# A decoder layer on one core: loads at the start split and reordered, the filter transformed by halves, and a new hand-found order

## The chip, the cores and the metric

The kernel runs on 1 core of a Trainium2 chip. The metric is the time of one execution on the device in microseconds (us), as the median of several runs; less is better.

## The reference

The input x has 4 batches of 1024 tokens of 256 values. The layer is a Hyena block, a cross attention with 16 heads over 64 context tokens, and a feed-forward block with ternary weights, each followed by a layer norm. What matters here is the Hyena block; `h` is a filter of full length for each of 2 orders and 256 channels:

```
t = linspace(0, 1, L)[:, None]                       # L = 1024
pe = sin(t * bands * 10)                             # 33 bands
h = sin(10 * (pe @ w1.T + b1)) @ w2.T + b2           # 64 hidden, 2 * 256 out
h = (h * exp(-exp(filt_decay) * t) + filt_bias) / L  # per order and channel
u = depthwise_conv3(x @ w_in.T + b_in)               # 768 channels: x0, x1, v
for n in range(2):
    y = irfft(rfft(v, 2L) * rfft(h[n], 2L))[:L]      # a long causal convolution
    v = y * u[n]
out = v.T @ w_out.T + b_out
```

## The kernel before, in words

**Units.** The Hyena part works on 8 units, a batch and a half of the 256 channels each (`units`, u = 0 to 7). Per unit: three projections (`stage_j`, which calls `project`: PE multiplies x by columns of `w_in`; ACT writes the middle tap of the three-tap convolution and the two outer taps into a pair of `tap` tiles; two adding DMAs issued by POOL put the outer taps onto the middle one). There are two pairs of tap tiles, so the third projection reuses the pair of the first, after its DMAs. Then `stage_tv` and `stage_tx` transpose on PE, `stage_f` transforms v by matmuls with the matrix `fw`, `stage_p` multiplies by the transformed filter `hf` on DVE, and `stage_i0`, `stage_i1` go back with the matrix `gi_`. `stage_f` takes one of two ways: the direct one, or *by fourths*, where `fourths` multiplies with a quarter of the matrix, and `join` makes the rest out of sums and differences on DVE. Which units go by fourths is the set `FOUR`. Attention and feed-forward follow from about 340 us on.

**The filter.** Before unit 0 can multiply, the filter must be there. `filter_basis`: two matmuls of 512 columns into `z`, a chain of seven DVE operations on `arg` and `kk` (64 partitions x 1024) that brings the argument of the sine into range, eight Exp on ACT for the decay (`dspace`, from the loaded `fdb`), one Sin into `saug`. `filters`: for each of eight pieces of 128 steps a matmul (`hp`), a multiplication and an addition on DVE (`hsb`). Then the transform: steps 0, 1, 4, 5 (even modulo 4) go by `fourths` and `join` in two halves of 256 columns (a half is one order); steps 2, 3, 6, 7 go directly, 16 matmuls of 512 columns, a copy on ACT and an addition and a subtraction on DVE for each quarter; a last operation (`stt`, the sign step) adds the even part to the odd. All fp32 matmuls appear in the profile as two MATMUL instructions each.

**PSUM.** `big1` hands out four slots of 1024 columns in a ring, in the order of the program's text. A later user of a slot waits until all readers of the earlier one are done.

**The order.** The kernel's calls are held as `Step`s and issued in an order which `plan` finds on the host: it keeps a clock for each engine with estimated costs (`Step.cost`), and among the steps that could start next on an engine it takes the one with the least rank. A rank is the place in the text (`nc.at`), an offset by stage, and a number out of the table `RANKS`, one for each task, a run of steps with the same stage and place. Queues are in order: each engine and each DMA queue (SP, ACT, POOL) executes what was issued first. Before the change all work ahead of the first loop is one task.

**The first loads.** On SP's queue: w1T, pv, x of batch 0 in two loads of 512 KB, then dftf into `fw`, dfti into `gi_` (1 MB each). On ACT's queue: peT, the first row of filt over 128 partitions (256 KB, into `vf`), all of w_in (768 KB), w2T, the second row of filt, w_out.

In the profile `pv`, `w_in`, `xt`, `fw`, `hf` go by their own names; the tiles `arg`, `kk`, `saug`, `hsb` lie in `x1sp`, the loaded filt and w2T in `vf`, the decay in `q`, `pe_sb` in `x1sp`, w1 in `pr`. All lines are L87, the line of the helper that issues the steps, so groups are told apart by tile names.

Of the kernel before, what the change touches and what calls it, by code (L numbers as in the profile page):

```python
# [16 lines left out]
P = 128  # L17
# [9 lines left out]
CALM = set(range(4))  # L27
MAGIC = 12582912.0
# [61 lines left out]
class Step:  # L90
# [23 lines left out]
    def cost(self):  # L114
# [23 lines left out]
        if self.engine == "ACT":  # L138
            return 0.1 + n * 0.00098 + 0.15 * (self.sum is not None), 0.15
        if self.what == "tensor_copy":  # L140
            return 0.1 + n * 0.00096, 0.06
        if n == 16:
            return 0.22, 0.06
        return 0.52 + n * 0.001 * (n > 64), 0.06
# [75 lines left out]
class Clock:  # L220


    def __init__(self, steps, before):
        self.steps, self.before = steps, before
        self.free = dict.fromkeys(("PE", "DVE", "ACT", "POOL", "SP"), 0.0)
        self.table, self.mode, self.wire = None, "", 0.0
        self.bank = [dict.fromkeys(self.free, 0.0) for _ in range(8)]
        self.end, self.start = [0.0] * len(steps), [0.0] * len(steps)
# [17 lines left out]
    def run(self, i, ready):  # L246
# [9 lines left out]
        end = t + s.us  # L256
        self.free[e] = self.end[i] = end
# [58 lines left out]
def follow(steps, before, order):  # L316
# [10 lines left out]
    43.1, -121.95, -51.3, 35.7, 0.75, -46.25, -78.7, 6.05, -35.75, 2.2, 13.15, -82.8, 19.9, -102.2, -24.45, -20.9,  # L327
    3.9, -39.65, 15.15, -30.9, 40.2, -28.15, -4.8, -32.9, -66.5, -63.2, 15.35, -47.35, -49.85, -1.05, 11.9, 113.35,
    -71.55, -36, 0.4, 18.1, 20.7, -127.8, -32.2, -163.5, -136.8, -61, -75.2, 2.45, 13.25, -16.05, 2.55, -56.1,
    29.55, 38.35, 49, -27.05, 39.65, 24.25, 1.1, 49.95, -15.6, -95.2, -44.2, -50.7, -61.1, 3.4, -50.4, -36.55,  # L330
    -45.15, 10.05, 50.2, -68.15, 14.9, -46.8, -12.85, 9.45, -18.3, 7.8, -61.5, -13.95, 16.55, -82.75, -45.55, -3.85,
    -89.85, -61.3, 65.3, -109.05, -50.75, -85.6, 17.3, -26.7, -34.85, 37.55, 22, 64, 30.8, 6, -89.45, -67.35,
    -66.05, -121.9, -45.1, -22.4, -9.75, -88, -44.25, -38.1, -22.55, -6.65, 0.85, -94.4, -15.8, -40.2, 43.1, 15,
    5.2, 4.85, 27.75, 35.05, -26.4, 13.2, 33.35, 95.6, 17.8, -0.25, 27.75, -79.9, -121.9, -56.85, 54.45, -47.5,
    -52.1, 9.4, -71.7, -5.25, -19.5, -27.4, -22.5, -19.45, -30.15, -32.9, 3.3, -56.15, 22.3, -16.55, 37.25, 12.15,
    -6.2, 96.55, -79.6, -76.7, -57.45, -14.4, -29.75, -38.3, -50.25, -98, -79.45, -33.2, -16.8, -11.9, -30.4, -30.85,
    -38.35, -4.95, -51.25, -58.15, -10.35, 9.7, -38.05, -6.35, -30.75, -7.75, -13.8, -13.95, -27.9, -10.3, -9.6, -12.25,
    -8.9, -10.3, 27.45, 21.55, -7.65, -38.25, -4.65, 36.05, -3.9, 44.25, -9.1, 42.95, -79.9, 29.45, -4.3, 24.9,
    -5.75, -3.9, -46.4, 13.5, -0.3, -1.55, -5.35, -2.55, -2.75, -1.1, 44.9, -1.5, 39, -32.4, -4, -2.9,
    -0.55, -4.6, -31.9, -0.45, -39.05, 14.05, -0.7, 1.35, -1.05, -12.9, 3.6, -0.5, -0.45, 120.35, 0.8, 0.95,  # L340
    2.65, 0.65, 4.95, -0.5, 29.3, 3.55, 1.55, -69.05, 1.35, 0, -37.8, -11.2, -8.45, -9.8, 5.5, 17.85,
    -1.8, -13.1, 1.25, -1.45, -0.6, -40.15, -0.65, -0.1, 24.55, -0.1, -6.75, -53.3, -1.35, -16.75, 0.85, 0.55,
    40.95, 0.95, -10.9, 0.65, -66.2, -33.15, 0.4, 1.2, 16.45, 5.35, -4.3, 0.35, 0.9, -5.85, 9.45, 15.75,
    12.75, 9.2, 35.5, -36.65, -5.45, 0.9, 1, -7.85, 0.05, -2.75, -3.15, 24.65, -31, -2, 1.3, -9,
    0.6, -0.3, 0.5, 53.1, 87.6, -0.35, -1.15, 1.2, -8.75, 0.35, 15.4, -30.5, 45.1, -0.45, -2.85, -4.6,
    -0.4, -78.8, 2.05, 12.05, 63.1, 57.45, 49.85, 19.35, 15.8, -1.35, -0, 15.55, 6.6, 60.3, 26.35, -1,
    -54.85, 12.05, -1.5, -30.8, -14.5, 22.3, 56.65, 34.75, 2.75, 0.2, -0.35, 4.9, 3.6, 45.6, -6.4, 27.8,
    -40.95, 3.65, -43.65, 7.4, 5, 37.8, 73.2, 8.35, 20.9, -15.55, 13.7, -65.45, -48.75, 18.7, 37.55, 30.55,
    -0.5, 2.9, -29.2, -48.75, -33.8, 38.9, 13.4, 0.85, -40.6, 5, -115.8, -43.15, -7.95, 12.5, 107.55, 26.3,
    -32.5, 21.85, -8.5, 8.4, -2.6, -13, 33.15, -29.25, -63.15, 23.55, 10.35, -63.55, -57.75, 4, 84.3, -53.25,  # L350
    -10, -73.5, -73.55, 17.65,
# [7 lines left out]
def decoder_kernel(  # L359
# [152 lines left out]
    def big1(name):  # L512
        return space_of["rest"]()

    if True:
# [9 lines left out]
        def load_x(b):  # L525
            xts[b] = xt_t.rearrange("p (k l) -> p k l", k=2)
            for kt in range(2):
                nc.sync.dma_start(xts[b][:, kt, :], xT[kt * P : kt * P + P, b * L : b * L + L])
# [9 lines left out]
        pe_sb, arg, kk, saug = spare[3][:33], spare[0][:64], spare[1][:64], spare[2][:65]  # L538
# [7 lines left out]

        nc.sync.dma_start(w1_sb, w1T)
        nc.scalar.dma_start(pe_sb, peT)
        nc.sync.dma_start(pv, pvec)
        load_x(0)  # L550
# [3 lines left out]
        nc.scalar.dma_start(w_in_sb, w_inT.rearrange("(k p) f -> p k f", p=P))  # L554
        nc.scalar.dma_start(w2_sb, w2T)
        nc.scalar.dma_start(fdb[:, 1, :], fd[:, 1, :])
        nc.sync.dma_start(fw, dftf.rearrange("(k p) f -> p k f", p=P))
# [11 lines left out]
        def filter_basis():  # L569
            z = big1("z")  # L570
            for h in range(2):
                mm(z[:64, h * 512 : h * 512 + 512], w1_sb, pe_sb[:, h * 512 : h * 512 + 512], start=True, stop=True)
            ts_(arg, z[:64, :], pv[:64, C_B1 : C_B1 + 1], 10.0, ALU.add, ALU.mult)
# [9 lines left out]
            act(saug[:64, :], arg, AF.Sin)  # L583

        def filters():

            hsb = [spare[4 + t // 2][:, t % 2 * 512 : t % 2 * 512 + 512] for t in range(8)]
# [5 lines left out]
            for half in range(2):  # L593
                n2 = slice(2 * half, 2 * half + 2)
                c2 = slice(256 * half, 256 * half + 256)
                ps = fourths(f"ha{half}", lambda par, q: hsb[4 * par + q][:, c2])
                h = hf[:, n2, 0]
                join(h.rearrange("p n c (s k d) -> p s c k n d", s=2, k=2), h[:, :, :, 0:256], h[:, :, :, 256:512], *ps)

            for cs in range(2):  # L600
                for kt in range(2):
                    m = (2 * cs + kt) * P
                    ha = big1(f"ha{cs}_{kt}")
                    for par in range(2):
                        for q in range(2):
                            mm(
                                ha[:, par * 512 : par * 512 + 512],
                                fw[:, 2 * par + q, m : m + P],
                                hsb[4 * par + 2 + q],
                                start=q == 0,  # L610
                                stop=q == 1,
                            )
                    ho = hospace[:, 2 * cs + kt]
                    nc.scalar.copy(ho, ha[:, 512:1024])

                    sg = C_SG + (cs + kt) % 2
                    for st, op in ((0, ALU.add), (1, ALU.subtract)):
                        f = slice(st * 256 + kt * P, st * 256 + kt * P + P)
                        h1, h0 = hf[:, :, 1, cs, f], hf[:, :, 0, 1 - cs, f]
                        tt_(h1, ha[:, 0:512].rearrange("p (n d) -> p n d", d=P), ho.rearrange("p (n d) -> p n d", d=P), op)  # L620
# [882 lines left out]
```

## Time and profile before

| | us |
|---|---|
| median of 3 runs | 681.19 (680.97 to 683.53) |
| the profiled execution, its own time | 683.8 |
| its span, first to last instruction | 682.0 |
| TensorE matmul (PE) busy | 629.3 |
| VectorE (DVE) busy | 605.2 |
| ScalarE (ACT) busy | 413.5 |
| GpSimd (POOL) busy | 201.9 |

The mean granted TensorE clock is 0.983 of full speed. The page gives each engine's busy time over the span; the same by stretches shows where in the span an engine is idle. The chain that ended last follows the work back from the last instruction to what released it. A group of instructions is told by engine, operation and tiles, with the number of instructions, the busy time and the mean length of one. Lengths of matmuls overlap, since they are pipelined: the distance from one to the next is shorter than the length.

### The profile page before, as it was taken

The numbers are of one execution on the slowest core, as the hardware profiler recorded it, in microseconds if no ns is written. First come the engines' busy times: TensorE is split into PE (matmuls) and PEld (weight loads), VectorE is DVE, ScalarE is ACT, GpSimd is POOL, SyncE is SP. The second block draws the span as 40 slices with busy tenths as digits, with TensorE's granted clock in tenths as the row PEclk, the third lists the DMA queues.
The fourth block names the chain that finished last, engine by engine and source line by source line (L and its number), as shares of the span: only waits on it lengthen the run. The fifth ranks groups of instructions, "written<-read, shape, count | busy, mean of one in ns | idle before, by whom it ended". The sixth has DMA issues, their size and how long they took to land.

```text
span 682.0 us, 12320 instructions
## 1 busy us (share of the span) xinstructions
PE 629.3 (92%) x4731; PEld 432.0 (63%) x4764; DVE 605.2 (89%) x1214; ACT 413.5 (61%) x626; POOL 201.9 (30%) x303
## 2 busy tenths in 40 slices
PE   4989799999999989999799998999999999999973
PEld 1445377777787667875577666756566666656642
DVE  4469859999989989999899899879998989989997
ACT  4623446538256855387132342598988898788871
POOL 1300313204132313374001224223333333533344
PEclk9989899999999989999799999999999999999999
DMA  8563848649596496965833130001211113413145
GB/s 279 97 105 123 169 83 149 124 98 183 120 166 113 69 209 113 172 115 100 187 116 83 51 62 2 3 16 33 48 40 40 41 48 50 93 48 56 40 78 131
DMA packets 65487, 65.71 MB, mean 96 GB/s; under 512 B 36660, under 2 KB 47284, under 8 KB 65430
## 3 DMA queue, kind: packets, MB, share of 16 engines
q0 software_dynamic: 17472, 35.66, 30.2%
q1 hardware_dynamic: 46044, 26.26, 14.8%
q10 hardware_dynamic: 1914, 3.02, 1.4%
q8 instruction: 37, 0.61, 0.4%
q14 instruction: 20, 0.16, 0.1%
HBM read 17.21 MB, written 4.19 MB: 31 GB/s over the span
## 4 chain that ended last, share of the span: by engine, by line
PE 61%; DVE 23%; DMA 5%; issue 4%; ACT 4%; POOL 2%; ACTq 0%; POOLq 0%; DVEq 0%
PE ps_t L87 61%; DVE t L87 5%; DVE q L87 5%; DVE small_t L87 4%; DMA xc<-tap 3%; DVE vf L87 2%; DVE xt L87 2%; DVE x1c L87 2%; DMA w_in<-in_w_inT 2%; ACT tap L87 1%; POOL ln_t L87 1%; DVE x1sp L87 1%; DVE ln_t L87 1%; ACT x1sp L87 1%; POOL small_t L87 1%
## 5 line engine op out<-in xcount | busy, mean ns | idle before, releaser
L87 PE MATMUL ps_t<-hf 128*128 128x512 bf16 (+1 forms) x479 | 98.4, 322 | 11.4 <-DVE x1c L87 3.8
L87 PE MATMUL ps_t<-xt,w_in 128*128 128x512 f32 (+1 forms) x200 | 90.8, 600 | 6.5 <-DMA w_in<-in_w_inT 5.4
L87 PE MATMUL ps_t<-vt,fw 128*128 128x256 f32 x384 | 90.9, 387 | 4.0 <-ACT tap L87 2.9
L87 POOL DMA_DIRECT2D xc<-tap x32 | 39.2, 1226 | 169.0 <-ACT tap L87 131.0
L87 PEld LDWEIGHTS ps_t<-vt,fw 128*128 128x128 f32 x384 | 72.9, 193 | 18.9 <-ACT tap L87 3.6
L87 PEld LDWEIGHTS <-hf 12*128 12x128 bf16 (+2 forms) x768 | 56.5, 97 | 40.0 <-issue 18.1
L87 DVE TENSOR_TENSOR t<-vf,hf 128x1024 f32<-128x1024 f32 x64 | 76.3, 1219 | 0.0
L87 ACT ACTIVATE tap<-ps_t,tbias,pv 128x1024 f32<-128x1024 f32 x48 | 55.9, 1209 | 20.7 <-DMA xc<-tap 20.7
L87 PEld LDWEIGHTS ps_t<-xt,w_in 128*128 128x128 f32 x200 | 38.2, 195 | 47.1 <-issue 43.6
L87 DVE TENSOR_TENSOR t<-t 128x1024 f32<-128x1024 f32 (+1 forms) x60 | 57.3, 973 | 1.5 <-DMA t<-q 1.4
L87 PE MATMUL ps_t<-q,gi__108 128*128 128x256 f32 x192 | 48.8, 401 | 6.6 <-DVE q L87 3.4
L87 PE MATMUL ps_t<-gi__108,q 128*128 128x256 f32 (+1 forms) x256 | 50.3, 352 | 1.7 <-DVE q L87 1.7
L87 POOL TENSOR_TENSOR small_t<-small_t,mhalf 128x1 f32<-128x1 f32 x64 | 35.8, 566 | 46.8 <-DVE small_t L87 46.4
L87 PEld LDWEIGHTS ps_t<-gi__108,q 128*128 128x128 f32 x256 | 43.9, 201 | 8.2 <-DVE q L87 2.1
L87 ACT ACT_TABLE_LOAD x34 | 43.6, 1283 | 7.2 <-DMA pv<-in_pvec 5.5
L87 PEld LDWEIGHTS ps_t<-q,gi__108 128*128 128x128 f32 x192 | 36.8, 200 | 17.6 <-DVE q L87 6.0
L87 PE MATMUL ps_t<-tap,hf 128*32 128x128 f32 (+1 forms) x896 | 44.3, 260 | 0.3
L87 DVE TENSOR_TENSOR q<-t 128x512 f32<-128x512 f32 x64 | 44.2, 730 | 0.1
L87 DVE TENSOR_REDUCE xt<-ps_t 128x16 f32<-128x1024 f32 x32 | 38.9, 1216 | 5.4 <-PE ps_t L87 3.9
L87 POOL COPY vf<-vf 128x1024 f16<-128x1024 f16 x32 | 33.2, 1038 | 29.6 <-DMA hf<-vf 10.3
L87 ACT ACTIVATE xc<-ps_t,cbias,pv 128x512 f32<-128x512 f32 x32 | 24.4, 776 | 27.2 <-PE ps_t L87 27.0
L87 DVE TENSOR_TENSOR q<-vf,hf 128x1024 f32<-128x1024 f32 x32 | 38.8, 1221 | 0.3
(149 smaller groups left out, 1350.0 us busy)
## 6 DMA issues: line engine op xcount, KB each, us to landing
xc<-tap POOLq DMA_DIRECT2D x32, 512.0 KB, 5.2
x1c<-tap POOLq DMA_DIRECT2D x16, 512.0 KB, 6.9
t<-q POOLq DMA_DIRECT2D x16, 512.0 KB, 6.4
xt<-in_xT SPq DMA_DIRECT2D x8, 512.0 KB, 6.2
out_y<-v SPq DMA_DIRECT2D x32, 128.0 KB, 1.7
x1sp<-in_x POOLq DMA_DIRECT2D x4, 512.0 KB, 5.8
x1sp<-in_x SPq DMA_DIRECT2D x4, 512.0 KB, 4.2
hf<-x1sp SPq DMA_DIRECT2D x3, 512.0 KB, 4.0
```

The lines of the kernel that those rows point to most:

```text
L87: pin(steps[i].f(*steps[i].a, **steps[i].k))
```

## The change

- x of batch 0 is loaded in four pieces, the first 512 columns of both channel halves first. w_in is loaded in two pieces: columns 512:768 second on ACT's queue, columns 0:512 after w2T and both rows of filt.
- `arg` and `kk` lie on 128 partitions x 512 instead of 64 x 1024; b1 is given twice. Sin is done in two pieces.
- The odd filter steps too go by `fourths` and `join` (FILT4); the sign step is done by halves.
- `filters` is split: `filter_steps` (the eight pieces `hsb`) and `filters(half)`. The pieces ahead of the loop get places of their own and stand in the text as: basis, first projection, filter steps, the other projections, half 0, transpose, transform of unit 0, half 1, second transpose.
- The planner's costs for ACT and POOL are other ones, it counts PE at half speed for 5 us after a pause of over 2.6 us, and `RANKS` is replaced as a whole.

```diff
+FILT4 = True
...
-            return 0.1 + n * 0.00098 + 0.15 * (self.sum is not None), 0.15
+            given = sum(self.k.get(w) is not None for w in ("bias", "scale") if not isinstance(self.k.get(w), float))
+            return 0.03 + n * 0.00087 + 0.105 * given + 0.19 * (self.sum is not None), 0.15
         if self.what == "tensor_copy":
-            return 0.1 + n * 0.00096, 0.06
-        if n == 16:
-            return 0.22, 0.06
-        return 0.52 + n * 0.001 * (n > 64), 0.06
+            return 0.1 + n * 0.00096 * (0.92 if n > 256 else 1.0), 0.08
+        if "pow" in str(self.a):
+            return 0.3 + 0.24 * n, 0.08
+        return 0.15 + n * 0.001 * (1.7 if self.what == "tensor_tensor" else 0.9), 0.06
...
         end = t + s.us
+        if e == "PE":
+            if t - self.free[e] > 2.6:
+                self.cold = t + 5.0
+            if t < self.cold:
+                end += s.us
...
 RANKS = [
-    43.1, -121.95, -51.3, 35.7, 0.75, -46.25, -78.7, 6.05, -35.75, 2.2, 13.15, -82.8, 19.9, -102.2, -24.45, -20.9,
+    16.9, -73.5, -17.05, 31.55, 7.65, -23.6, 88.7, -49.5, 12.3, 45.75, 30.85, 103.15, -0.3, 8.7, 65.05, 21.35,
...
         def load_x(b):
             xts[b] = xt_t.rearrange("p (k l) -> p k l", k=2)
-            for kt in range(2):
-                nc.sync.dma_start(xts[b][:, kt, :], xT[kt * P : kt * P + P, b * L : b * L + L])
+            for h in range(2 if b == 0 else 1):
+                c = slice(512 * h, 512 * h + 512) if b == 0 else slice(0, L)
+                for kt in range(2):
+                    nc.sync.dma_start(xts[b][:, kt, c], xT[kt * P : kt * P + P, b * L : b * L + L][:, c])
...
-        pe_sb, arg, kk, saug = spare[3][:33], spare[0][:64], spare[1][:64], spare[2][:65]
+        pe_sb, arg, kk, saug = spare[3][:33], spare[0][:, 0:512], spare[1][:, 0:512], spare[2][:65]
...
         nc.scalar.dma_start(pe_sb, peT)
         nc.sync.dma_start(pv, pvec)
+        nc.scalar.dma_start(w_in_sb[:, :, 512:768], w_in3[:, :, 512:768])
         load_x(0)
...
         nc.scalar.dma_start(fdb[:, 0, :], fd[:, 0, :])
-        nc.scalar.dma_start(w_in_sb, w_inT.rearrange("(k p) f -> p k f", p=P))
         nc.scalar.dma_start(w2_sb, w2T)
         nc.scalar.dma_start(fdb[:, 1, :], fd[:, 1, :])
+        nc.scalar.dma_start(w_in_sb[:, :, 0:512], w_in3[:, :, 0:512])
...
-                mm(z[:64, h * 512 : h * 512 + 512], w1_sb, pe_sb[:, h * 512 : h * 512 + 512], start=True, stop=True)
-            ts_(arg, z[:64, :], pv[:64, C_B1 : C_B1 + 1], 10.0, ALU.add, ALU.mult)
+                mm(z[64 * h : 64 * h + 64, 0:512], w1_sb, pe_sb[:, h * 512 : h * 512 + 512], start=True, stop=True)
+            ts_(arg, z[:, 0:512], pv[:, C_B1 : C_B1 + 1], 10.0, ALU.add, ALU.mult)
...
-            act(saug[:64, :], arg, AF.Sin)
+            for h in range(2):
+                act(saug[:64, 512 * h : 512 * h + 512], arg[64 * h : 64 * h + 64], AF.Sin)
...
-            for half in range(2):
-                n2 = slice(2 * half, 2 * half + 2)
-                c2 = slice(256 * half, 256 * half + 256)
-                ps = fourths(f"ha{half}", lambda par, q: hsb[4 * par + q][:, c2])
-                h = hf[:, n2, 0]
+        def filters(half):
+
+            n2 = slice(2 * half, 2 * half + 2)
+            c2 = slice(256 * half, 256 * half + 256)
+            for a in range(2 if FILT4 else 1):
+                ps = fourths(f"ha{half}_{a}", lambda par, q: hsb[4 * par + 2 * a + q][:, c2])
+                h = hf[:, n2, a]
                 join(h.rearrange("p n c (s k d) -> p s c k n d", s=2, k=2), h[:, :, :, 0:256], h[:, :, :, 256:512], *ps)
...
-        nc.at = -40 - 13 * (NU - 2) - 10
-        filter_basis()
-        stage_j(0)
-        filters()
-        stage_tv(0)
-        stage_f(0, 0)
-        stage_tx(0)
+        nc.at = -40 - 13 * (NU - 2) - 20
+        for piece in (
+            filter_basis,
+            lambda: stage_j(0, 0),
+            filter_steps,
+            lambda: stage_j(0, 1, 2),
+            lambda: filters(0),
+            lambda: stage_tv(0),
+            lambda: stage_f(0, 0),
+            lambda: filters(1),
+            lambda: stage_tx(0),
+        ):
+            piece()
+            nc.at += 1
...
-    b1[:64, 0] = i["L0_attn_b1"]
+    b1[:, 0] = np.tile(i["L0_attn_b1"], 2)
```

## The prediction, before the result was known

> **What bounds the kernel now.** I read the head of the page first, then the busy time of the engines by stretches, then the chain that ended last over the first 60 us, then the instructions in order of time from 0 to 110 us, and last what each engine waited for.
>
> ```profile
> span 682.0 us, 12320 instructions
> PE 629.3 (92%) x4731; PEld 432.0 (63%) x4764; DVE 605.2 (89%) x1214; ACT 413.5 (61%) x626; POOL 201.9 (30%) x303
> ```
>
> TensorE (PE) stands still for only 52.7 us, VectorE (DVE) for 76.8. Two engines close to full: what one loses, the other soon asks for. So the place of the idle time counts. By stretches (us, then busy time and instructions of PE, PEld, DVE, ACT, POOL, then granted clock, DMA share, GB/s):
>
> ```profile
> 0.00:12.50 12.50, 3.64 (x4) 0.73 (x4) 6.27 (x9) 6.93 (x10) 3.14 (x23) 1.00 0.76 242
> 12.50:26.50 14.00, 13.96 (x27) 6.14 (x28) 1.85 (x2) 7.65 (x9) 1.41 (x1) 1.00 0.44 149
> 26.50:69.00 42.50, 39.46 (x123) 22.57 (x122) 36.13 (x63) 14.98 (x18) 6.00 (x5) 0.96 0.57 122
> 69.00:100.00 31.00, 25.87 (x91) 17.39 (x90) 21.16 (x23) 13.67 (x16) 7.20 (x6) 0.89 0.69 136
> 100.00:310.00 210.00, 204.68 (x858) 153.62 (x857) 199.26 (x239) 123.20 (x188) 67.44 (x58) 0.99 0.73 134
> 310.00:340.00 30.00, 24.29 (x102) 17.30 (x101) 27.61 (x35) 13.88 (x17) 7.33 (x7) 0.89 0.75 155
> 340.00:640.00 300.00, 290.62 (x3347) 198.20 (x3375) 274.73 (x732) 209.53 (x338) 91.03 (x171) 1.00 0.22 49
> 640.00:682.00 42.00, 26.82 (x189) 16.06 (x190) 38.18 (x116) 23.70 (x34) 18.38 (x34) 0.98 0.39 91
> ```
>
> From 100 to 310 PE is busy 97% and DVE 95%; there is little to find. To 100 us PE idles 17.1 of its 52.7 us, DVE 34.6 of its 76.8. The change works exactly there. The chain shows why (start, length, what):
>
> ```profile
> 1.79 10.62 DMA w_in<-in_w_inT
> 12.54 6.26 PE ps_t L87 x8
> 18.82 0.78 ACT xc L87
> 19.61 1.28 ACT L87
> 20.91 1.06 ACT x1sp L87
> ...
> 24.04 5.23 DMA xc<-tap
> 29.56 6.21 DMA xc<-tap
> ...
> 35.85 1.22 ACT tap L87
> 37.11 21.82 PE ps_t L87 x60
> ```
>
> The first projection waits for all of w_in (12.40 us); ACT's Sin for the filter (20.91) stands behind an evacuation of that projection; DVE's first filter step follows only at 26.55. Then the third projection's tap buffer waits for two adding DMAs in a row, and the filter steps wait for its PSUM.
>
> **The change part by part.**
>
> *Loads.* x of batch 0 comes in four pieces of 256 KB, first halves first; w_in's columns 512:768 (256 KB) come second on ACT's queue, the other 512 KB behind w2 and both filt loads. Before, x's two 512 KB loads landed 7.0 and 10.1 us after issue at 1.7 and 2.1, at about 8.7 and 12.2. The same bytes now put both first halves at about 8.7, so the first projection starts there, not at 12.54: 3.8 us earlier on PE. Its second half still waits for 12.2. Price: one more issue on ACT's queue (w_in's took 0.45 us) and two on SP's (0.4 us each) ahead of dftf and dfti, which are needed at 30 and 77 us. The first filt load now queues behind 256 KB: w_in's 768 KB took the 5.65 us from 6.75 to 12.40, so a third is 1.9 us, and the eight Exp end at 14.3, not 12.4. The other w_in columns land at about 16 (w_out, last on that queue before, landed at 16.1); the projections that need them come after the first filter steps in the new text.
>
> The row says the 16 engines were busy at a share of 0.95 to 1.05 from 6 to 18 us, with pieces of 128 KB to 1 MB in line. The Trainium skill, "DMA: Bandwidth & Descriptors", section "Bandwidth", says the opposite of splitting: batch to 1 MiB, each transfer having some 2 us of fixed cost. By that rule three more transfers would cost up to 6 us if each stood alone; with the engines full as here I leave it out of the sum.
>
> *Filter argument on 128 partitions.* DVE's chain on 64x1024 (1.28 + 1.41 + 3.72 + 0.68 = 7.1 us from 7.19 to 14.38) becomes 128x512, half of it, 3.5 us less. It is hidden: Sin came at 20.91 after it. Sin splits into two of 64x512 (512-column rows on ACT are 0.63 each): 1.3 us against 1.06.
>
> *Restart of DVE.* Exp to 14.3, table load 1.28, Sin 1.3: 16.9. In the trace the first filter MATMUL started at 25.48 and DVE at 26.55, 1.07 later: so DVE restarts at 18.0 instead of 26.55, 8.6 us earlier. If ACT evacuates the first projection ahead of Sin (2 x 0.78 + 2.28 = 3.8 us), it is 21.8, 4.8 earlier. I take the first, since the projection's second half only ends near 15.
>
> *Odd filter steps by fourths.* Out go 32 MATMULs of 512 columns (24 such took 10.46 us: 0.436 each, 13.9); in come 32 of 256 (16 took 3.72: 0.233 each, 7.4). PE saves 6.5 us. On ACT four copies at 0.587 become two at 1.013: nothing. DVE loses 8 additions (5.2 busy) and gains what the two joins of the even steps cost: 2.6 + 2.3 + 0.8 + 2.4 + 2.6 = 10.7 busy. The eight sign steps of 512 columns (5.6) become sixteen of 256: between 0.35 each (half) and 0.47 (a 256-column row of this operation from PSUM), 5.6 to 7.5; I take 0.42, the 256-column addition's row, so +1.1. DVE net: 10.7 - 5.2 + 1.1 = **+6.6 us**. It lies on the engine that has the chain from 63.84 to 80.5, so it is paid in full.
>
> *Order by halves.* The filter steps now take their PSUM ahead of projections two and three, so the wait for the tap DMAs no longer stands before them: DVE's idle of 3.33 (38.27) and 1.91 (41.61) goes, 5.2 us; PE's 2.4 too. Half 1 of the filter (about 14 us on DVE) is not needed by unit 0, only by unit 1's first product near 99 us. It can fill DVE's 7.73 us of idle before 90.65: between 0 and 7.7; I take half, 3.9, because half 1 stands before unit 0's second transpose and all of unit 1 in the ring of PSUM slots, so part of it must run early.
>
> *Sum of the front, on DVE:* -8.6 + 6.6 - 5.2 - 3.9 = **-11.1** (from -7.2 to -14.9). *Check on PE:* 3.8 (start) + 6.5 + 2.4 = 12.7, and up to 3.9 more, since nine MATMULs of the first projection ran at about 0.86 us against 0.43 later. In the trace they stayed slow from 12.54 to 17.7, 5.2 us, after a pause of 5.4. The Trainium skill, "TensorE: Matmul & The Clock Gate", section "Part 1", gives some 3.4 us for warming and for cooling; the trace's 5.2 is longer, and by the page a pause of 1.6 us (7.15 to 8.7) would leave earned warmth in place, worth up to those 3.9. PE allows the 11.1, so DVE decides.
>
> *All ranks new, and other costs in the planner.* No row prices a new order. Bounds: the one large stall past 100 us is at 310 to 340, where the projection's DMA issue (321.13) sat behind others on POOL and PE idled 5.7 us and lost 11% of its clock, 3.3: 9.0 us. Losing it gains 9.0, another one like it costs 9.0. The planner's old figure for the four-wide power on POOL was 0.52 us, the new one 1.26, the row 1.59; ACT's were below the 1.14 at which scaled 1024-column rows follow each other, and now meet it. An order from better figures is likelier to lose the stall than to add one; I take a third, **-3**.
>
> Total -14.1. The profiled execution took 683.8 us (span 682.0 and 1.8 around it), 2.6 above the median of 681.19. 683.8 - 14.1 = 669.7; taken from the median, **667.1 us**.
>
> **Rivals.**
> 1. *Everything is found.* Front -14.9, the stall at 310 gone (-9.0), and some of the tail's DVE work (38.2 of the last 42 us, while DVE idles 25.3 from 340 to 640) moved forward, say -5: -28.9, **652.3**. For it: that idle exists. Against: PE is full there.
> 2. *DVE swallows the gain.* Sin behind the evacuation (-4.8), +6.6, -5.2, nothing filled: -3.4, order neutral: **677.8**, on the edge of no change. For it: DVE was busy 17.7 of the 20 us after 40.
> 3. *The loads don't arrive earlier,* because the engines are full and share alike: PE starts at 12.5 as before. PE's 12.7 shrinks to 8.9, with the order's 3: **669.3**.
> 4. *Slower: the new order makes waits behind POOL's adding DMAs,* whose issues sit in one queue and take 5.2 to 6.9 us to land. Place: a projection whose issue stands behind another's, as at 321. Price 9.0 each; with the front at its weak end (-7.2) it decides from two more such stalls: -7.2 + 18 = +10.8, **692.0**. Against it: one in 540 us so far.
>
> **How the numbers follow.** Half a per cent, 3.4 us, is about what a measurement of this kernel tells from no change. Forecast (660 to 677) 0.50; rival 1 (650 to 660) 0.24; rival 3 0.06; rival 2 0.11, of which 0.02 falls just below 677.8; rival 4 0.09. So faster 0.82, same 0.09, slower 0.09. The range, 652 to 682, leaves out rival 4, the far half of rival 1 and the edge of rival 2.
>
> **What would show it.** Right, if the first MATMUL of a projection starts near 8.7, Sin near 15 to 17, DVE's first filter product near 18 (22 in rival 2), and the first product of v and filter near 50 to 58 instead of 68.94; if the fw MATMULs on the filter are 64 of 256 columns; and if no wait of 5 us or more for an adding DMA is left before 100. Wrong, if DVE idles as much from 18 to 100 as it did from 26.55 (16.2 us), if PE's busy time does not fall by 6 to 10 us, or if PE's idle time past 100 us (35.6) moves by more than 9 either way: then the order decided, not the front.

## The result, and the profile after

The changed kernel takes 684.35 us (679.91 to 688.67, 20 executions), the kernel before 681.14 (679.95 to 683.53, 20): a ratio of 1.0046, 95% interval 1.0027 to 1.0064. It is a little slower, where 667.1 was forecast. The profiled execution happened to be the longest of the 20, with its own time of 688.67 and a warm clock of 0.949, where every other profile here has 1.00; a second profile of the same program (`after_again`, own time 683.55, clock 1.00 when warm) is read beside it. Ratios leave out executions over 1.5% above the shortest of the same kernel; below this concerns `half_late_new_rest` alone, with four.

The head of the page, and the engines by the same stretches as before (us; busy time and instructions of PE, PEld, DVE, ACT, POOL; granted clock, DMA share, GB/s):

```profile
span 686.9 us, 12384 instructions
...
PE 640.7 (93%) x4764; PEld 436.5 (64%) x4764; DVE 611.6 (89%) x1232; ACT 421.6 (61%) x631; POOL 202.4 (29%) x303
...
PEclk8998699999999999999999999999999999999986
```

```profile
0.00:12.50 12.50, 6.32 (x10) 1.94 (x10) 5.24 (x10) 3.29 (x5) 3.13 (x23) 0.99 0.80 259
12.50:26.50 14.00, 12.72 (x27) 5.85 (x28) 5.46 (x9) 11.15 (x15) 1.41 (x1) 0.84 0.58 165
26.50:69.00 42.50, 37.32 (x128) 23.64 (x126) 39.65 (x73) 20.37 (x22) 7.20 (x6) 0.91 0.58 123
69.00:100.00 31.00, 24.73 (x89) 17.79 (x90) 21.84 (x27) 10.47 (x11) 7.27 (x6) 0.80 0.65 132
100.00:310.00 210.00, 207.02 (x844) 152.04 (x842) 195.53 (x233) 120.05 (x184) 66.28 (x56) 0.95 0.71 132
310.00:340.00 30.00, 23.51 (x109) 16.14 (x109) 27.49 (x38) 16.79 (x24) 7.66 (x7) 0.95 0.81 174
340.00:640.00 300.00, 295.37 (x3367) 199.75 (x3369) 275.91 (x724) 215.70 (x340) 90.77 (x169) 0.95 0.22 47
640.00:686.90 46.90, 33.69 (x204) 19.38 (x196) 40.52 (x125) 23.76 (x34) 18.70 (x36) 0.81 0.35 82
```

Add up PE's first four rows: 81.1 of 100 us, so PE idles 18.9 us up to 100. Before it was 17.1. PE had 6.8 us less to do there (the `fw` matmuls on the filter went from 8.4 + 13.9 to 15.5) and started 5.2 us earlier, and yet its idle time grew by 1.8. The clock fell as well (the PEclk row in tenths for 40 slices, and the column behind the busy times): 0.84, 0.91 and 0.80 in the three rows from 12.5 to 100, where before it was 1.00, 0.96 and 0.89. The 1.00 needs care: before's records of the clock begin at 17.7 us, and its MATMULs from 12.54 up to there start 0.85 us apart, those behind it 0.43. (PE's busy time of the two pages can't be set against each other: the page of before lacks 33 MATMUL records (x4731 beside x4764 weight loads), and a matmul at half clock counts as busy for twice as long.)

The front did start earlier. The chain of waits over the first 60 us, in order of time (start, length, what):

```profile
5.00 8.74 DMA w_in<-in_w_inT
...
13.78 16.20 PE ps_t L88 x38
...
40.72 3.87 PE ps_t L88 x16
...
50.09 5.29 DVE hf L88 x13
55.39 0.07 DVE q L88
...
56.44 3.62 DVE hf L88 x5
```

The wait for w_in is still at the head of it, now for its columns 0:512. The first product of v and filter comes at 55.30, not 68.94: 13.6 us gained. But look at the last two lines: one piece of product (`q`), and the chain is on `hf` again. DVE's instructions from there (start, length, engine, line, operation, tiles, shapes, number; in brackets the idle time before):

```profile
55.30 1.22 DVE L88 TENSOR_TENSOR q<-vf,hf 128x1024 f32<-128x1024 f32 x1
56.44 1.22 DVE L88 TENSOR_TENSOR hf<-hf 128x1024 f32<-128x1024 f32 x1
...
67.04 3.25 DVE L88 SCALAR_TENSOR_TENSOR hf<-hf,pv 128x256 f32<-128x256 f32 x8
70.21 1.21 DVE L88 TENSOR_TENSOR t<-t 128x1024 f32<-128x1024 f32 x1
71.35 1.22 DVE L88 TENSOR_TENSOR q<-vf,hf 128x1024 f32<-128x1024 f32 x1
...
87.12 1.22 DVE L88 TENSOR_TENSOR vt<-ps_t,x0t 128x1024 f32<-128x1024 f32 x1 [7.37 <-PE ps_t L88]
...
95.16 1.23 DVE L88 TENSOR_TENSOR q<-vf,hf 128x1024 f32<-128x1024 f32 x1
```

Before, the same instructions stood like this:

```profile
68.94 1.23 DVE L87 TENSOR_TENSOR q<-vf,hf 128x1024 f32<-128x1024 f32 x1
70.09 2.35 DVE L87 TENSOR_TENSOR t<-vf,hf 128x1024 f32<-128x1024 f32 x2
...
73.49 1.22 DVE L87 TENSOR_TENSOR q<-vf,hf 128x1024 f32<-128x1024 f32 x1
...
90.65 1.23 DVE L87 TENSOR_TENSOR vt<-ps_t,x0t 128x1024 f32<-128x1024 f32 x1 [7.73 <-PE ps_t L87]
...
98.97 1.22 DVE L87 TENSOR_TENSOR q<-vf,hf 128x1024 f32<-128x1024 f32 x1
```

Now half 1 of the filter stands between unit 0's products. The second `q` of unit 0 begins at 71.35, against 73.49 before, and unit 1's first at 95.16, against 98.97. Of 13.6 us, 2 to 4 are left. PE has nothing meanwhile:

```profile
54.78 12.60 PE L88 MATMUL ps_t<-xt,w_in 128*128 128x512 f32 x24 [2.08 <-DVE hf L88]
73.22 2.08 PE L88 MATMUL ps_t<-q,gi__108 128*128 128x256 f32 x4 [5.84 <-DVE q L88]
77.35 7.00 PE L88 MATMUL ps_t<-q,gi__108 128*128 128x256 f32 x20 [2.06 <-DVE q L88]
```

And DVE's idle of 7.73 us at 90.65, which half 1 was to fill, is still there: 7.37 ahead of 87.12.

### The profile page after: what moved, and what is told of

Same layout as the page of the kernel before. It is cut to its first block, busy times and chain, and to the rows that moved or that the text cites. A ratio compares the mean times of both kernels' runs of the same rounds, so it can differ in the third digit from the quotient of the medians.

```text
span 686.9 us, 12384 instructions
## 1 busy us (share of the span) xinstructions
PE 640.7 (93%) x4764; PEld 436.5 (64%) x4764; DVE 611.6 (89%) x1232; ACT 421.6 (61%) x631; POOL 202.4 (29%) x303
## 4 chain that ended last, share of the span: by engine, by line
PE 72%; DVE 13%; ACT 5%; DMA 5%; issue 3%; POOL 1%; ACTq 0%; POOLq 0%; SPq 0%; DVEq 0%
PE ps_t L88 72%; DVE t L88 3%; DMA xc<-tap 3%; DVE hf L88 2%; ACT tap L88 2%; DVE small_t L88 2%; DVE q L88 2%; DMA w_in<-in_w_inT 1%; DVE xt L88 1%; ACT x1sp L88 1%; DVE vf L88 1%; DVE v L88 1%; POOL ln_t L88 1%; DVE x1c L88 1%; ACT pr L88 0%
## 5 line engine op out<-in xcount | busy, mean ns | idle before, releaser
L88 PE MATMUL ps_t<-hf 128*128 128x256 f16 (+1 forms) x512 | 109.0, 342 | 8.1 <-DVE x1c L88 2.7
L88 PE MATMUL ps_t<-xt,w_in 128*128 128x512 f32 (+1 forms) x200 | 97.6, 634 | 8.0 <-DMA w_in<-in_w_inT 2.1
L88 PEld LDWEIGHTS <-hf 12*128 12x128 bf16 (+2 forms) x768 | 58.6, 100 | 42.8 <-issue 19.2
L88 PE MATMUL ps_t<-q,gi__108 128*128 128x256 f32 x192 | 51.1, 413 | 9.6 <-DVE q L88 9.6
L88 POOL COPY vf<-vf 128x1024 f16<-128x1024 f16 x32 | 33.4, 1044 | 43.2 <-ACT vf L88 15.7
L88 DVE TENSOR_TENSOR q<-t 128x512 f32<-128x512 f32 x64 | 42.7, 702 | 0.1
```

The lines of the kernel that those rows point to most:

```text
L88: pin(steps[i].f(*steps[i].a, **steps[i].k))
```

## The experiments

**The kernels.** To change one thing at a time, most kernels take the order of steps as a written list in place of the planner: a *front* up to the last step of the filter and of unit 0's transposes, behind it the *rest*, which has the same steps in both kernels. "Old rest" is before's list, "new rest" the changed kernel's. Where a front was found anew, the planner searched ranks for the front's tasks alone.

The table puts three landmarks of each profiled execution beside the times: the first product of v and filter of unit 0, of unit 1, and the first of order 1 (unit 0's second order), the first that needs half 1. The last column is the span less that third landmark.

| kernel | median us (range, runs) | ratio to before, 95% | unit 0 | unit 1 | order 1 | span behind it |
|---|---|---|---|---|---|---|
| before | 681.14 (679.95 to 683.53, 20) | 1 | 68.94 | 98.97 | 116.08 | 565.9 |
| changed (`after_again`) | 686.11 (683.55 to 687.67, 6) | 1.0074 (1.0053 to 1.0094) | 57.27 | 96.55 | 113.64 | 568.1 |
| `front_new_rest_old` | 681.14 (677.77 to 685.20, 12) | 0.9998 (0.9976 to 1.0021) | 57.52 | 97.75 | 114.86 | 565.7 |
| `front_old_rest_new` | 686.57 (684.95 to 689.59, 6) | 1.0080 (1.0056 to 1.0104) | 68.03 | 100.71 | 117.81 | 566.5 |
| `new_front_direct_odd` | 680.20 (676.65 to 686.42, 12) | 0.9979 (0.9956 to 1.0002) | 65.94 | 98.28 | 115.38 | 564.5 |
| `loads_alone` | 679.54 (677.79 to 681.12, 12) | 0.9967 (0.9953 to 0.9982) | 67.22 | 97.00 | 114.11 | 563.5 |
| `new_front_old_loads` | 679.20 (677.85 to 679.61, 10) | 0.9957 (0.9942 to 0.9971) | 55.31 | 96.09 | 113.19 | 563.0 |
| `keep_warm` | 682.75 (676.92 to 686.71, 12) | 1.0003 (0.9976 to 1.0031) | 54.63 | 94.94 | 112.04 | 566.6 |
| `half_late` | 675.31 (673.39 to 677.18, 6) | 0.9907 (0.9880 to 0.9934) | 56.86 | 90.12 | 107.22 | 566.4 |
| `front_searched` | 677.56 (673.11 to 679.24, 6) | 0.9932 (0.9908 to 0.9956) | 60.32 | 93.13 | 110.23 | 565.9 |
| `half_late_right` | 670.56 (668.48 to 677.25, 6) | 0.9859 (0.9825 to 0.9894) | 61.88 | 80.71 | 111.69 | 563.8 |
| `half_late_old_loads` | 674.75 (673.69 to 675.70, 4) | 0.9899 (0.9886 to 0.9913) | 55.94 | 73.08 | 108.89 | 565.0 |
| `half_late_direct` | 682.07 (678.21 to 683.30, 11) | 1.0003 (0.9990 to 1.0017) | 64.66 | 94.45 | 113.79 | 565.9 |
| `half_late_warm` | 671.02 (669.62 to 673.03, 5) | 0.9845 (0.9822 to 0.9868) | 53.65 | 72.47 | 103.47 | 564.3 |
| `half_late_new_rest` | 682.11 (672.93 to 684.35, 12) | 0.9935 (0.9898 to 0.9972) | 53.46 | 72.28 | 103.27 | 570.8 |
| `half_late_direct_free` | 682.55 (681.69 to 685.70, 12) | 1.0018 (1.0003 to 1.0033) | 62.44 | 88.75 | 115.10 | 568.4 |

Read the last two columns first: with the old rest a kernel needs 563 to 568 us from the first product of order 1 on, whatever its front was (each from one execution). So that landmark tells, to some 5 us, what a front is worth, and unit 0's, by which the prediction went, does not.

**1. Which half of the change: the front or the order behind it?** The changed kernel again, and the two mixed ones (a list has over 5000 numbers; here it is told in words).

```diff
-    (order from the planner and RANKS)
+ORDER = front steps of the changed kernel's list, then before's list     # front_new_rest_old
+ORDER = before's front steps, then the changed kernel's list             # front_old_rest_new
```

> The changed kernel once more, for a profile at the clock that most of its executions have. Theory 1 (VectorE's added work takes the front's head start back by 95 us, and the new order past it loses the rest): 681 to 683 us at a mean clock of about 0.975, and the trace shows a warm clock of 1.00 past 100 us, with the first product of unit 1 again some 4 us ahead of before. Theory 2 (the order gained, but TensorE's clock took it): the clock past 100 us is again near 0.95 and the time 685 to 689.

> The changed kernel up to its last filter step, then all later steps in the order that the kernel before issues them in. Theory 1: the head start of 3.8 us that is left at unit 1's first product (98.97 to 95.16) comes through: 677 us, from 675 to 679. Theory 2: the clock is low here too, 684 or more. Theory 3 (the front gains nothing that the later, full engines don't take): 680 to 682, as before.

> The kernel before up to its last filter step, then all later steps in the order of the changed kernel. Theory 1: the new order past the front costs what the changed kernel lost between 95 us and its end at equal clock, about 4 us: 685, from 683 to 687. Theory 2: the order is no worse, 679 to 682 where the clock is full.

Measured: 686.11, 681.14 and 686.57. The new front is worth nothing, and the new order costs 5 us with either front. The largest change in PE's waits lies from 300 to 340 us. PE's waits there in `after_again`, then in the new front with the old rest:

```profile
308.04 3.20 PE L88 MATMUL ps_t<-q,gi__108 128*128 128x256 f32 x8 [2.56 <-DVE q L88]
...
325.21 3.36 PE L88 MATMUL ps_t<-vt,fw 128*128 128x256 f32 x8 [4.78 <-ACT tap L88]
...
336.43 0.70 PE L88 MATMUL ps_t<-xt,w_in 128*128 128x256 f32 x2 [0.98 <-ACT hf L88]
```

```profile
310.30 3.03 PE L88 MATMUL ps_t<-q,gi__108 128*128 128x256 f32 x12 [0.71 <-DVE q L88]
324.61 3.67 PE L88 MATMUL ps_t<-xc,w_in 128*128 128x512 f32 x8 [1.62 <-DVE vf L88]
331.54 1.98 PE L88 MATMUL ps_t<-ident,xc 128*128 128x128 f32 x8 [3.26 <-DMA xc<-tap]
```

The wait for the adding DMA (3.26) is gone, but one of 4.78 for ACT's tap evacuation and one of 2.56 for DVE have come: 8.3 us of waits against 5.6 with the old rest. The stall was moved, not lost. A part of the 4.78 is ACT's own queue: ahead of the evacuation at 322.19 it issues two loads for the attention, from 319.56 on (0.37 and 1.83 us). From 400 on PE's waits of 0.9 us or more sum to 7.1 us there and to 5.6 with the old rest.

These waits don't add up to the 5 us, though. Over all of the span behind 100 us PE idles 32.2 us in `after_again` and 32.6 with the old rest, and the two profiled executions are only 1.2 us apart (683.55 and 682.40). In the mean of the timed executions the new order has more time at half clock (experiment 3 says how that is counted): 39.9 us against 31.5 with the new front, 25.4 against 18.4 with the old one. That the order costs 5 us is shown by the exchange; where it loses them stays open.

**2. The odd steps and the loads, each alone.** `new_front_direct_odd` sets `FILT4 = False` in the new front, ordered anew for it, with the old rest. `new_front_old_loads` is that front with before's loads; `loads_alone` is before's program and order with the split loads.

> As the new front with the old rest, but with the odd filter steps done directly (FILT4 off; the planner orders the front anew for it). VectorE has about 5.5 us less to do, TensorE 6.5 more. Theory 1 (VectorE sets the front to unit 1's first product): that product comes 2 to 5 us earlier than with fourths, and the time is 673 to 677. Rival (TensorE sets it): up to 6.5 us later, 680 to 684.

> The kernel before in its own order, with only the loads of x and w_in split and reordered as in the change. The first projection starts at 7.3 us instead of 12.54, the other two wait for the rest of w_in until about 13.8; they end at about 21 instead of 25.5, and everything in the front comes some 4 us earlier. Theory 1 (what comes early on both engines is kept): 677 to 678. Rival (a wait further on, for the adding DMAs at 24 to 36 us, ends as late as before): 680 to 682.

> The new front with the old rest in the same order, but with the loads of before: x in two pieces, w_in in one ahead of w2. The first projection waits until about 12.5 again, the Exp start some 3 to 4 us earlier, since the second row of filt and w2 no longer wait behind anything but w_in. If the loads are what moved the filter up (theory 1): 3 to 5 us slower than with the new loads, 684 to 686. If VectorE's start after Sin sets it, which the split loads delay: the same or faster, 679 to 681.

Measured: 680.20, 679.54, 679.20. Undoing the fourths changes nothing (681.14 to 680.20, overlapping intervals), though unit 0's product moves from 57.5 to 65.9: one more sign that that landmark doesn't count. Since its front was ordered anew, this weighs the edit and a search together. The split loads gain 0.33% in before's order and cost 2 to 3 us in the new front (1.9 by the medians, 2.8 by the ratios). The profiles differ in PE's start: with the split PE gets ahead of ACT, waits 1.5 us for its tap at 20.5, and has 6.8 us at half clock from 23.2; with the old loads it waits once, to 12.0, and has no half clock ahead of 56. In the changed kernel's own profile the split has another pause, 2.1 us at 11.7 for the other columns of w_in.

**3. The clock.** In the records of the granted clock, before's profile has 20.4 us at half clock ahead of 670, `after_again`'s 27.3, in pieces of 3.4, 6.8 or 13.7 us that begin within a pause of PE or up to 2 us behind one. From the mean clock of each timed execution, the time at half clock is 2 x (1 - clock) x span: about 18 us for before (0.987), 39 for the changed kernel (0.964 to 0.978, without the execution at 0.929), 31 for the new front with the old rest. `keep_warm` puts eight matmuls, whose results are overwritten, into the wait of 7.3 us at 69.

```diff
+            if u == 0 and parts[0] == 0:
+                for _ in range(8):
+                    mm(ps[:, 0:512], ident, fw[:, 0], start=True, stop=True)
```

> The new front with the old rest, and eight more matmuls of 512 columns, of no use to the result, into the free PSUM slot ahead of unit 0's first inverse transform. They lie in the 7.3 us in which TensorE waits for VectorE from 69.3 us and take 7.0 us at full clock; the matmuls behind them are the same. Theory 1a (the pauses in the front put TensorE at half clock, 10.2 us of it from 74.4, and that eats what is saved): the stretch at half clock shrinks to 3.4 us or none, unit 0's inverse transform runs at 0.22 us a matmul instead of 0.43, and the time falls by 2 to 4 us against the new front with the old rest (681.1): 677 to 679, at a mean clock of 0.982 or more. Rival (VectorE sets the pace there, and the clock costs nothing): 681, or some tenths more.

Measured: 682.75, no gain, with the executions spread over 10 us. Within the 12 the time follows the clock (676.92 at 0.991, 686.71 at 0.976), but filling one pause doesn't set it: in its profile the wait at 69 is gone, and half-clock pieces of 3.4 us stand at 13.6, 54.6 and 78.4. Inconclusive on the cause. What holds is the correlation: over the timed executions of the changed kernel, but for the profiled one, and of the 15 experiments, each taken against its own kernel's mean, one us more at half clock goes with 0.37 us more time (from -0.10 to 0.54 by kernel). By this the 21 us more at half clock of the changed kernel are **7.7 us**. The execution left out, at 0.929, was only 4.3 us above its kernel's median; with it the figure is 0.24, and the 7.7 become 5. That it is cause and not company, no run here proves.

**4. Half 1 of the filter late.** A look at `stage_p` shows which half a product reads: `nh = 2 * n + dh`, so half 1 is order 1, first needed at 112 to 116 us. `half_late` puts it between two parts of unit 0's inverse transform.

```diff
-            lambda: filters(1),
...
             stage_i0(u, 0, 1, 2)
             weights(u, "i")
+            if u == 0:
+                nc.at += 0.5
+                filters(1)
+                nc.at -= 0.5
```

> The new front and the old rest, but the second half of the filter stands behind the start of unit 0's inverse transform in the text, and the steps up to there are ordered anew, so that VectorE works through unit 0's products first. Theory 1b (the second half's 14 us on VectorE between unit 0's products take the head start back): TensorE's wait at 69.3 goes, the first product of unit 1 comes at 88 to 93 us instead of 97.75, and the time is 674 to 678. Rival (the engines past 100 us take it whatever the front does): the product comes earlier, and the time stays at 680 to 682.

Measured: 675.31. In this kernel the fourth PSUM slot of half 1 is the one that unit 0's inverse transform still holds, so that unit's values are overwritten; the time may be too good for want of a wait, or too bad. So it was done again in a place where no slot of unit 0 is open, beside a control in which the same search leaves half 1 where the change put it.

```diff
-            lambda: filters(1),
...
             stage_tx(u + 1)
+            if u == 0:
+                nc.at += 0.5
+                filters(1)
+                nc.at -= 0.5
```

> The changed program with half 1 of the filter where the change put it, the front's order searched anew (the same search as for the next kernels), before's order behind it: the control for them. Theory (the place of half 1 and the pauses cost the gain, not the way the order was found): 679 to 683 us like the new front with the old rest (681.1); the first product of unit 1 at 94 to 98. Rival (a better search alone gives the 5.8 us of half 1 late): 674 to 677, first product of unit 1 near 90.

> As the control, but half 1 of the filter stands in the program behind unit 1's second transpose, where no slot of unit 0 is open, and before's order follows its last step. Theory: half 1's 14 us of DVE work leave the time before unit 1's first product, which comes at 82 to 92 (control 94 to 98); PE's wait of 7.3 us for DVE near 69 goes or halves, and the time is 671 to 677. Rival 1 (what half 1 late gained came from the slot that it overwrote, whose wait was missing): 679 to 683. Rival 2 (PE is full past 100, so the work only moves): unit 1's first product early, but PE waits as long for DVE at 90 to 130, and 678 to 682.

Measured: 677.56 for the control, **670.56** for half 1 late. The search alone gives 3.6 us, more than the theory allowed (681.14 to 677.56), and the place of half 1 another 7.0 (5.0 by the ratios, 0.9932 to 0.9859, whose intervals lie apart). Each of the two fronts was searched once, and a search alone is worth 3.6, so the size is rough. The direction is not: the four kernels with half 1 late, fourths and the old rest took 670.56 to 675.31, the four with half 1 early, fourths and the old rest 677.56 to 682.75. The stretch from 69 to 100 shows it; the control, half 1 late, and `half_late_warm` (experiment 5), which has half 1 in the same place and a clock of 1.00 here:

```profile
69.00:100.00 31.00, 29.24 (x103) 19.71 (x104) 27.78 (x40) 11.26 (x13) 5.93 (x6) 0.89 0.70 136
```

```profile
69.00:100.00 31.00, 31.00 (x114) 22.44 (x113) 31.00 (x42) 11.84 (x13) 5.98 (x5) 0.92 0.61 131
```

```profile
69.00:100.00 31.00, 30.17 (x118) 21.69 (x118) 30.96 (x45) 14.41 (x16) 4.82 (x4) 1.00 0.59 138
```

With half 1 late PE and DVE are both busy for all or nearly all of the 31 us; in the changed kernel they were 24.73 and 21.84. Unit 0's products stand ahead of half 1 (61.88, 66.43), unit 1's begin at 80.71, and half 1, but for one operation at 78.64, falls from 88.66 on among the last of them and ahead of the first product of order 1. PE idles 12.9 us up to 100, against 18.0 in the control and 18.9 in the changed kernel. The control's waits of PE for DVE's `q` from 55 to 80 us (in all, times, the longest) are gone, and one for ACT's `vt` at 65.2 has come:

```profile
PE ps_t L88 <- DVE q L88: 6.1, 3, 4.3
```

```profile
67.97 6.76 PE L88 MATMUL ps_t<-vt,fw 128*128 128x256 f32 x16 [2.76 <-ACT vt L88]
```

That this execution has its third landmark only at 111.69 goes with the clock: it was the longest of the six (677.25), with 17.1 us at half clock in one piece from 19.5; `half_late_warm`, without that piece, has it at 103.47.

**5. The remaining parts, with half 1 late.**

> As half 1 late in its right place, with the loads of before. Theory (in the new front the split only lets PE start and then pause at 11.7 for 2.1 us, worth -2 for the old loads): first projection near 12.4, no pause until unit 0's projections are done, and 669 to 675, 1 to 3 us below half 1 late with split loads. Rival (the 2 us belonged to that order): equal within 1 us or slower by 1 to 3.

> As half 1 late in its right place, with steps 2, 3, 6, 7 of the filter direct as before (32 matmuls of 512 columns instead of 32 of 256). Theory (with half 1 out of the way PE is the limit to 100): PE's 6.5 us more show in part, 2 to 5 us slower than half 1 late. Rival (DVE still decides, and 5.4 us less work on it pay): 0 to 3 us faster.

Measured: 674.75 for the old loads, 4.2 slower than with the split loads by the medians, 2.7 by the ratios, whose intervals overlap a little. The theory (1 to 3 faster) failed: what the old loads gained in experiment 2 belonged to that front. `half_late_direct` (682.07) says little: the copies of its odd steps lie in the tile of unit 1's transformed v, which they overwrite, so unit 1's product had to wait for half 1 (94.45). Hence three more, each against `half_late_right`. `half_late_warm`:

```diff
+            if u == 0 and ct == 4:
+                for h in (0, 1):
+                    mm(ps[:64, 0:512], w1_sb, pe_sb[:, h * 512 : h * 512 + 512], start=True, stop=True)
...
+                if t == 0:
+                    for _ in range(3):
+                        mm(hp[:, 0:512], w_in_sb[:, 0, 512:640], xts[0][:, 0, 0:512], start=True, stop=True)
```

`half_late_new_rest` changes the list behind the front; `half_late_direct_free` puts the copies in the tile `vo`, which unit 0 needs only shortly ahead of order 1, in two places by turns instead of four:

```diff
-FILT4 = True
+FILT4 = False
...
-                        ho = hospace[:, 2 * cs + kt, 0:256]
+                        ho = vo_t[:, (2 * cs + kt) % 2 * 256 : (2 * cs + kt) % 2 * 256 + 256]
```

> Half 1 late in its right place, with matmuls whose results are overwritten put into PE's two pauses of the start: two of the filter's argument ahead of the first projection (2.0 us into the pause of 1.8 at 5.6) and three of x by w_in ahead of the first filter step (2.8 us into the pause of 2.6 at 16.1). No result changes. Theory (the pauses make the half-clock stretch of 6.8 to 17 us that follows at 19.5, and so the spread of 668.5 to 677.3): mean clock 0.987 or more in nearly all executions, none above 673, median 667 to 670. Rival (the half clock comes and goes whatever PE does here): the same spread of clocks, 0.977 to 0.992, and 670 to 673 with the 1 us of matmuls that stick out.

> Half 1 late in its right place up to the last step of the filter, behind it the changed kernel's own order instead of before's. Theory (the new order itself costs time past the front): 4 to 6 us slower than half 1 late with before's order, 674 to 677. Rival (the new order only suffered from the new front's place of half 1): 668 to 672.

> Half 1 late in its right place with steps 2, 3, 6, 7 direct, their copies in a tile that nothing else holds then (in the run before they lay in unit 1's transformed v, which waited for them and was overwritten). Theory: TensorE and VectorE are both full from 69 to 100, so PE's 6.5 us more cost 2 to 5 and DVE's 5.4 us less give back nothing: 672 to 676. Rival (DVE decides): 667 to 670.

*The warm front*: 671.02, the same as without. PE's first matmuls in it, and the one of `half_late_right` that stood behind the pause:

```profile
3.62 5.35 PE L88 MATMUL ps_t<-x1sp,pr 33*64 33x512 f32 x8 [3.62 <-DMA pr<-in_w1T]
8.90 10.31 PE L88 MATMUL ps_t<-xt,w_in 128*128 128x512 f32 x18
19.05 7.03 PE L88 MATMUL ps_t<-vf,x1sp 65*128 65x512 f32 x16
```

```profile
18.73 13.20 PE L88 MATMUL ps_t<-vf,x1sp 65*128 65x512 f32 x16 [2.60 <-issue]
```

The same 16 matmuls took 13.20 at half clock and 7.03 without the pauses, and no piece at half clock stands ahead of 58 us in this profile (span 667.8, against 675.5). But the first projection starts 1.5 us later behind the added matmuls, and two of its five executions still had a clock of 0.981. The longest is 673.03 instead of 677.25; the mean 671.3 instead of 672.0. With five and six executions that suggests, no more, that the pauses of the front make the long executions and not the usual ones; as a means to a better median the theory failed.

*The new rest*: five executions took 672.9 to 675.9 and seven 681.8 to 684.4, the former at clocks of 0.976 to 0.984, the latter at 0.967 to 0.974. By the ratios (0.9935 to 0.9859) the new rest costs 5.2 us, by the medians 11.6; the better group alone has its median 2.5 above `half_late_right`'s. So the new order costs time behind this front too, and the clock falls more often: its profile has 3.4 us at half clock at each of PE's pauses of 2.5 (294.9), 4.5 (309.9), 2.2 (400.1) and 1.8 us (640.6).

*The direct odd steps*: 682.55, 12 us slower than by fourths (11 by the ratios). Both theories missed it, the first (2 to 5 slower) in size alone. PE's 6.5 us more of work can't make 12. Three more things differ, and no run parts them: the front was searched anew, the copies share two places (at 101.87 ACT has waited 2.24 us for DVE's `hf`), and the mean clock was 0.976 against 0.984. In its profile DVE waits 4.35 us for ACT's `vo` at 113.78, just ahead of the first product of order 1. Where half 1 was early, the same edit was worth nothing. That fourths pay once PE is the limit fits both results, but is not shown.

## Why the prediction was wrong, point by point

- **What bounds the kernel, and that the front can give**: right. The front was priced at -11.1 from before; `half_late_right` has the changed loads, argument, fourths and halves with before's rest, and is 11.0 below the executions of before on the same chip (681.61 to 670.56; 9.6 by the means). The sum was of the right size for a front that the changed kernel doesn't have. That the two agree so closely is partly luck: 3.6 of it is the search.
- **Loads**: the first projection started at 7.33, earlier than the 8.7 forecast. What was left out: six matmuls later it stops for 2.1 us, because the w_in columns 0:512 landed at 13.74 and the second projection stood ahead of the filter steps, not behind them as the text of the program has it.
- **Restart of DVE** at 18.0: 21.00 in the first profile, 18.53 in the second; Sin came at 17.44 and 16.67 (forecast 15 to 17). Right in the second. The first lost 2.5 us: w_in landed 0.9 later, and the ten MATMULs behind it took 6.1 us instead of 4.5, with a piece at half clock from 13.7.
- **Odd steps by fourths**: PE -6.8 (forecast -6.5), DVE +6.4 (its operations on `hf` up to 125 us, 41.1 to 47.5; forecast +6.6). Right as work. That PE's gain would be of use failed: PE's idle time rose.
- **Order by halves, the step that failed.** "Half 1 ... is not needed by unit 0, only by unit 1's first product near 99 us. It can fill DVE's 7.73 us of idle." It is needed by unit 0, but only by its second order, at 112 to 116; and it filled nothing. It lay in the middle of unit 0's products, where PE waited for DVE 7.9 us in two waits. From the first filter product to 100 DVE idled 12.1 us instead of 16.2: 4.1 less, where 5.2 + 3.9 were booked; in the second profile it was 15.7, only 0.5 less. The reason for booking half of the 7.7 was that "part of it must run early". All of it ran early, and that cost more than the 3.9 booked: 5.0 to 7.0 us between the control and half 1 late.
- **"PE allows the 11.1"**: failed as well. The check counted PE's work and no pause. PE's idle time to 100 went from 17.1 to 18.9, and the time at half clock from 18 to 39 us, a term of some 5 to 8 us, by the correlation alone, that the sum lacked. The check even allowed up to 3.9 us of gain on the clock; in the second profile the first six MATMULs of the projection took 5.15 us, 0.86 each, as slow as before.
- **All ranks new, -3**: wrong in sign, +5. The wait of 3 us for the adding DMA went, as hoped, but two others took its place; these are not the 5 us, whose place is open.
- **Rivals**: 2 (DVE swallows the gain, 677.8) names the engine rightly, not the mechanism; the front with the old rest came out at 681.1. Rival 4's waits behind POOL's adding DMAs did not come (in the changed kernel PE waits 0.4 us in all for one); those that came are on ACT and DVE.
- **The signs to look for**: first MATMUL near 8.7, Sin, unit 0's product at 50 to 58, 64 `fw` matmuls of 256 columns: all came true or nearly so (7.33, 17.44, 55.30), and the kernel was slower. They watched the start of the gain, none of them its end. Of the signs of being wrong, PE's busy time spoke: it did not fall by 6 to 10 us (629.3 before, 640.7 and 628.4 in the two profiles, as far as the missing records allow). PE's idle time past 100 us moved by less than the 9 (35.6 to 27.3 and 32.2), so that sign did not point at the order, which cost 5 us all the same.

In sum, forecast and measurement lie 17.3 us apart (-14.1 and +3.2). The place of half 1 is 5 to 7 of it and the order 8 (+5 instead of -3). The 2 to 4 left are of the size of what the search of the front alone found (3.6) and aren't settled further. The runs come from several chips, and the changed kernel was 3.2 slower in one set and 4.5 in another, so this is a rough sum. The 5 to 8 of the clock are not added to it, since the pauses belong to half 1's place and to the new order; that they lie within these two is argued, not measured. Open stays why filling pauses moves the median so little while the clock and the time go together within each kernel.

## What to carry to other kernels

A head start is worth what is left of it at the landmark from which nothing differs any more: find that landmark, here the first product that needs the last piece of the preparation, and ask of each piece which instruction reads it first and what the engine's queue puts ahead. When work is split so that a part can come later, look whether the program's order of buffers lets it come later; if it doesn't, it sits in the middle of the urgent work. And count pauses of TensorE, not only its busy time: here they came with pieces at half clock, and executions with more of these took longer, though filling single pauses did not move the median.

## What the runs showed of the hardware that was not expected

- Pieces at half clock are multiples of 3.4 us (3.4, 6.8, 10.2, 13.7, 17.1). They came with pauses of as little as 1.5 us (20.5 to 22.0 in the new front with the old rest: 6.8 us at half clock from 23.2) and 2.1 (52.7 to 54.8 in the changed kernel: 3.4 from 54.7), and one program had 17.1 us in one execution where its mean clock in another leaves no more than 11 in all. The Trainium skill, "TensorE: Matmul & The Clock Gate", section "Part 1", has the clock fall after an idle window of some 3.4 us; the pauses of 1.5 to 2.6 us here are shorter than that.
- One of 20 executions of the changed kernel was granted 0.949 where all other profiles show 1.00 when warm, from 10 us to the end (573 us of it in one piece), on a single core. The time was the longest of the 20, 688.67.
